# First pass of a two-layer attention block: full-array products of a step in one row, sums of exponentials counted a step later

## The chip, the cores and the metric

The kernel runs on one core of one Trainium2 chip. The metric is the device time of the program in microseconds. The median of three runs of the kernel before is 4034.56 us (4032.42 to 4036.78).

## What is computed

The input x has 8 images of 256 channels and 64 x 64 pixels, in float32. Two layers follow each other. The first, which the change concerns, is attention with keys and values from a reduced image:

```python
xr = conv(x, w_sr, stride 4)            # 256 tokens per image
xr = layer norm of xr over channels
q = w_q @ x
k, v = split(w_kv @ xr)
sim = q . k / sqrt(32)                  # 8 heads of 32 channels, 4096 queries, 256 keys
out = softmax(sim) @ v
x2 = x + gamma * (w_out @ out)
```

The second layer is linear attention on x2: a product with `w_qkv` (768 x 256), a 5 x 5 depthwise convolution with a small mixing, sums of k times v, their application to q, and a projection that is added to x2.

## The kernel before, in words

The program has three passes. `first_pass` does the first layer, the product with `w_qkv`, and some preparation of weights; `second_pass` does the convolution and the sums; `third_pass` applies them. A fourth part, `general`, is run only if sums in the softmax were out of range, which these data never bring. Engines are called PE (TensorE), DVE (VectorE), ACT (ScalarE), POOL (GpSimd) and SP (SyncE, which issues the DMAs).

The first pass walks through 256 steps. The list `order` runs over image `b` (8), block `s` of 512 pixels (8), half `c` of the channels, that is four heads (2), and half `kc` of the keys, that is 128 (2). So an image is a batch of 32 steps, even steps have kc = 0 and odd steps kc = 1, and two steps make one (s, c). The work is spread over steps as in a pipeline. In step n, with m = n - 1:

- `scores` (L770) multiplies q by k for step n. Each of four heads uses 32 rows of the array (L774, tile `sc`); the four results take four of the five PSUM banks that carry the tag `mm`. ACT takes the exponentials (L780) into tiles `e`, of which there are 12, that is three steps.
- `valued` (L788) multiplies the exponentials of step m by v (L793). Each head uses 32 columns of the array. The result `av` has a PSUM bank of its own and collects both halves of the keys.
- `joined` (L802), in odd steps, lets POOL add the exponentials of both halves, head by head (L804), into those of the first half.
- `counted` (L806), when m is odd, multiplies these by a matrix of ones, 32 columns per head (L809). The result `den`, also in a PSUM bank of its own, holds the sums of the exponentials, each 32 times.
- `normed` (L811) follows at once: ACT copies av to `att` (L817); DVE transposes den (L819), takes the reciprocal of one copy of each sum (L820), spreads it back by a transpose (L822) and multiplies att by it (L824). Two small ACT activations (L830) note the sums for the range check; they are put into the list `late`.
- `queries` makes q for the step after next, in even steps (L759, copied by ACT at L767).
- `added` (L836), in every fourth step, for the block whose last scores came three steps before, multiplies two att by `w_out` (L840, four full-array products in two banks `mm`), adds x on DVE (L841) and stores x2.
- After every second block, `differences` (L850) and the seven products of `qkv` (L870), three times over, are put into the table `todo`, for the next seven steps with 2, 3, 4, 1, 4, 3 and 4 products (the 21 products of a Strassen scheme). Their results, in banks `mm`, are copied by ACT (L947) or combined by DVE (L898, L901, L954, L958, L967), and partly transposed (L905, with a copy to `stage` at L911); both transposes and stores go through `late`. `new_stage` (L862) gives the buffer of a plane, whose border POOL clears (L864, L865).
- `keys_values` (L675) makes keys and values of the next image. It is a generator and is advanced in steps 12 to 26 of each batch, with the strided convolution (L687, tile `sr`) in the first eight of these.
- `conv_weights` (L654) prepares weights of the second pass in the first 32 steps: DVE multiplies into the one buffer `wb` (L663), which is stored by DMA.

What stands in `late` is run after the next step's scores. The products in `todo` come before `valued` in odd steps and after it in even steps. The instructions of each engine are issued in the order of this loop, except where the framework's scheduler moves them; `keep_in_program_order` marks those that it may not move. A read of a tile waits for its write by a semaphore, and a new use of a buffer waits for the last reader of the old one.

Of the kernel before, what the change touches and what calls it, by code (L numbers as in the profile page):

```python
# [27 lines left out]
F32 = mybir.dt.float32  # L28
AF = mybir.ActivationFunctionType
ALU = mybir.AluOpType  # L30
AX = mybir.AxisListType

P = 128
# [12 lines left out]
QB = 512  # L46
# [528 lines left out]
def first_pass(ctx: ExitStack, tc: tile.TileContext, a, fine, planes, x2d, kd, vd, wtd):  # L575
    nc = tc.nc
# [8 lines left out]
    rest = ctx.enter_context(tc.tile_pool(name="rest", bufs=2))  # L585
# [14 lines left out]
    def load_x(b):  # L600
        x_tiles[b] = xpools[b % 2].tile([P, 2, HW], F32, tag="x", name=f"x_{b}")
        for s in range(NG):
            load_strip(b, s)
# [42 lines left out]
    def border(b):  # L646
        v = vd[b].rearrange("n y x e -> y x n e")
        src = nil.rearrange("p (n e) -> p n e", n=8)
        for i in (0, NB2 + 1):
            nc.sync.dma_start(v[i], src)  # L650
            nc.sync.dma_start(v[1 : NB2 + 1, i], src[:NB2])
# [104 lines left out]
    def queries(b, s, c):  # L756
        ps = bank(f"q_{b}_{s}_{c}")
        for ci in range(2):
            nc.tensor.matmul(  # L759
                ps,  # L760
                consts["wq"][:, ci, c * P : (c + 1) * P],
                x_tiles[b][:, ci, s * QB : (s + 1) * QB],
                start=(ci == 0),
                stop=(ci == 1),
            )
        qs = two.tile([P, QB], F32, tag="q", name=f"q_{b}_{s}_{c}")
        nc.scalar.copy(qs, ps)  # L767
        return qs

    def scores(b, s, c, kc, qs):  # L770
        scs = [bank(f"sc_{b}_{s}_{c}_{kc}_{h}") for h in range(4)]
        for h in range(4):
            rows = slice(h * D0, (h + 1) * D0)
            nc.tensor.matmul(  # L774
                scs[h], kks[b][rows, c, kc * P : (kc + 1) * P], qs[rows], start=True, stop=True
            )
        es = []
        for h in range(4):
            e = two.tile([P, QB], F32, tag="e", name=f"e_{b}_{s}_{c}_{kc}_{h}", bufs=E_BUFS)
            nc.scalar.activation(e, scs[h], AF.Exp, scale=D0**-0.5)  # L780
            es.append(e)
        return es

    sums = {}

    late = []

    def valued(b, s, c, kc, es):  # L788
        if kc == 0:
            sums["av"] = psum_early.tile([P, QB], F32, tag="av", name=f"av_{b}_{s}_{c}")  # L790
        for h in range(4):
            cols = slice(h * D0, (h + 1) * D0)
            nc.tensor.matmul(  # L793
                sums["av"][cols],
                vvs[b][:, kc, c * P + h * D0 : c * P + (h + 1) * D0],
                es[h],
                start=(kc == 0),
                stop=(kc == 1),
            )


    def joined(es0, es1):  # L802
        for h in range(4):
            nc.gpsimd.tensor_tensor(es0[h], es0[h], es1[h], ALU.add)  # L804

    def counted(b, s, c, es):  # L806
        sums["den"] = psum_early.tile([P, QB], F32, tag="den", name=f"den_{b}_{s}_{c}")
        for h in range(4):
            nc.tensor.matmul(sums["den"][h * D0 : (h + 1) * D0], ones_w, es[h], start=True, stop=True)  # L809

    def normed(b, s, c):  # L811
        av, den = sums["av"], sums["den"]
        i = 2 * ((b * NG + s) * 2 + c)
        att = rest.tile([P, QB], F32, tag="att", name=f"att_{b}_{s}_{c}", bufs=4)
        turn = rest.tile([P, NB, D0], F32, tag="rden", name=f"rden_{b}_{s}_{c}", bufs=1)
        one = two.tile([P, NB], F32, tag="one", name=f"one_{b}_{s}_{c}")
        nc.scalar.copy(att, av)  # L817

        nc.vector.transpose(turn.rearrange("p n d -> p (n d)"), den)  # L819
        nc.vector.reciprocal(one, turn[:, :, 0])  # L820
        r = rest.tile([P, NB, D0], F32, tag="rall", name=f"rall_{b}_{s}_{c}", bufs=1)
        nc.vector.transpose(r, one.unsqueeze(2).to_broadcast([P, NB, D0]))  # L822
        r = r.rearrange("p n d -> p (n d)")
        nc.vector.tensor_mul(att, att, r)  # L824

        def noted():
            for k, t in enumerate((turn[:, :, 0], one)):
                copy = two.tile([P, NB], F32, tag="copy", name=f"copy_{b}_{s}_{c}_{k}")
                tc.keep_in_program_order(
                    nc.scalar.activation(copy, t, AF.Copy, accum_out=seen[:, i + k : i + k + 1])  # L830
                )

        late.append(noted)
        return att

    def added(b, s, att, oc):  # L836
        xt, cols = x_tiles[b], slice(s * QB, (s + 1) * QB)
        ps = bank(f"o_{b}_{s}_{oc}")
        for c in range(2):
            nc.tensor.matmul(ps, consts["wout"][:, c, oc * P : (oc + 1) * P], att[c], start=(c == 0), stop=(c == 1))  # L840
        nc.vector.scalar_tensor_tensor(  # L841
            xt[:, oc, cols], ps, consts["gam"][:, 0:1], xt[:, oc, cols], ALU.mult, ALU.add
        )
        nc.sync.dma_start(x2d[b][oc * P : (oc + 1) * P, cols], xt[:, oc, cols])
# [5 lines left out]
    def differences(b, g):  # L850
        xt = x_tiles[b]
        x = xt[:, :, 2 * g * QB : 2 * (g + 1) * QB].rearrange("p c (h n) -> p c h n", h=2)
        b11, b12, b21, b22 = (x[:, c, h] for c in range(2) for h in range(2))
        t = halves.tile([P, 4, QB], F32, tag="differences", name=f"differences_{b}_{g}", bufs=1)
        t1, t2, t3, t4 = (t[:, i] for i in range(4))
        nc.vector.tensor_sub(t1, b12, b11)
        nc.vector.tensor_sub(t2, b22, t1)
        nc.gpsimd.tensor_tensor(t3, b22, b12, ALU.subtract)
        nc.vector.tensor_sub(t4, t2, b21)
        quarters[b, g] = b11, b21, b22, t1, t2, t3, t4  # L860
# [126 lines left out]
    first = queries(0, 0, 0)  # L987
# [1 line left out]
        pass  # L989
    load_x(1)  # L990
    order = [(b, s, c, kc) for b in range(B) for s in range(NG) for c in range(2) for kc in range(2)]
    q, es, att = {0: first}, {}, {}
    ahead = iter(())

    def qkv_lazy(b, g, pair):
        made = []

        def go(i):
            def run():
                if i == 0:  # L1000
                    made.extend(qkv(b, g, pair))
                made[i]()

            return run

        return [go(i) for i in range(7)]

    n_all = len(order)
    todo = {}
    for n in range(n_all + 16):  # L1010
        m = n - 1
        if n < n_all:
            b, s, c, kc = order[n]
            es[n] = scores(b, s, c, kc, q[n // 2])
        was, late[:] = list(late), []
        for f in was:
            f()


        if n % 2:  # L1020
            for f in todo.pop(n, ()):
                f()
        if 0 <= m < n_all:
            valued(*order[m], es[m])
        for f in todo.pop(n, ()):
            f()
        if n < n_all and kc == 0 and n + 2 < n_all:
            q.pop(n // 2 - 1, None)
            q[n // 2 + 1] = queries(*order[n + 2][:3])
        if 0 <= m < n_all and order[m][3] == 1:  # L1030
            counted(*order[m][:3], es.pop(m - 1))
            es.pop(m)
            att[order[m][:3]] = normed(*order[m][:3])
        if n < n_all and kc == 1:
            joined(es[n - 1], es[n])
        if n >= 6 and (n - 6) % 4 == 0 and (n - 6) // 4 < B * NG:
            b, s = (n - 6) // 4 // NG, (n - 6) // 4 % NG
            for oc in range(2):
                added(b, s, [att[b, s, 0], att[b, s, 1]], oc)
            if s % 2:  # L1040
                differences(b, s // 2)
                products = [p for pair in (1, 2, 0) for p in qkv_lazy(b, s // 2, pair)]
                for i, count in enumerate((2, 3, 4, 1, 4, 3, 4)):
                    todo[n + 1 + i] = products[:count]
                    products = products[count:]
        next(weights, None)
        if n < n_all:
            b, at = n // 32, n % 32
            if at == 2:
                border(b)  # L1050
            if b + 1 < B:
                if at == 10 and b > 0:
                    load_x(b + 1)
                if at == 12:
                    ahead = keys_values(b + 1)
                if 12 <= at < 20:
                    next(ahead)
                    next(ahead)
                elif at >= 20:
                    next(ahead, None)  # L1060
# [688 lines left out]
```

## Time and profile before

| | |
|---|---|
| median of three runs | 4034.56 us |
| profiled execution, its own time | 4043.45 us |
| its span (first to last instruction) | 4041.7 us |
| busy: PE / DVE / ACT / POOL | 3954.6 / 2250.5 / 1511.8 / 1275.2 us |
| first score row of batches 1 to 7 | 321.9, 583.6, 840.7, 1098.0, 1355.1, 1612.3, 1869.6 us |
| first and last score row of the pass | 54.0 and 2088.3 us |
| additions of exponentials, L804 | 512 of 1.27 us (median) |

A float32 product of 512 columns appears as two records of a weight load (PEld) and two of a matmul (PE). The timeline joins records of one form that follow each other: a line has the start in us, the time from first start to last end, engine, line, operation, output and inputs, the part of the array used (128*128 is all of it, 32*128 a quarter of the rows, 128*32 a quarter of the columns), the tile's shape and the number of records; in brackets stand the idle time before it and what ended that. The list of waits has who waited for whom, then the sum in us, how often, and the longest. The lines by stretch give start and end, the length, busy time and instructions of PE, weight load, DVE, ACT and POOL, then the granted clock, the share of the DMA engines and GB/s. The page's slices cut the span into 40 parts and give tenths.

### The profile page before, as it was taken

The page shows a single profiled execution, that of the slowest core. Times are in us where ns is not written, and L with a number is a line of the kernel's source. Part 1 is how long each engine was busy: PE and PEld are TensorE (multiplying, and loading weights), DVE is VectorE, ACT ScalarE, POOL GpSimd, SP SyncE. Part 2 cuts the span into 40 slices and gives each one's busy share as a digit, 9 for nine tenths or more (in the row PEclk, how much of TensorE's full clock was granted, in tenths as well). Part 3 has the DMA queues.
Part 4 walks back from the last instruction along what each step waited for, and adds up shares of the span by engine and source line. Part 5 has one row for each costly group of instructions (what it writes and reads, how often), then busy time and mean ns, then how long its engine had stood idle before and what let it go on. Part 6 is the DMA issues. An engine that isn't in the chain of part 4 may idle for free. (4 is left out here: it accounts for less than half of the span.)

```text
span 4041.7 us, 70298 instructions
## 1 busy us (share of the span) xinstructions
PE 3954.6 (98%) x27074; PEld 2260.2 (56%) x27074; DVE 2250.5 (56%) x3752; ACT 1511.8 (37%) x3473; POOL 1275.2 (32%) x1394
## 2 busy tenths in 40 slices
PE   8999999999999999999997999999999998999999
PEld 4333433434334343343335888888888886556555
DVE  2576465564655645555664566666666664444443
ACT  2334344343443434434432222222222223555444
POOL 2334233343343433424433344444444440000000
PEclk9999999999999999999998999999999998999999
DMA  7655444435344353434548878778778756767674
GB/s 236 186 172 144 143 105 145 103 98 155 93 141 112 96 157 93 134 105 107 137 111 237 247 223 235 221 219 236 222 219 233 208 167 173 229 197 235 196 235 138
DMA packets 569897, 691.37 MB, mean 171 GB/s; under 512 B 60112, under 2 KB 429264, under 8 KB 565328
## 3 DMA queue, kind: packets, MB, share of 16 engines
q1 hardware_dynamic: 569552, 686.78, 60.0%
q8 instruction: 215, 3.52, 0.4%
q14 instruction: 130, 1.06, 0.1%
HBM read 412.54 MB, written 274.10 MB: 170 GB/s over the span
## 5 line engine op out<-in xcount | busy, mean ns | idle before, releaser
L804 POOL TENSOR_TENSOR e<-e,e 128x512 f32<-128x512 f32 x512 | 656.2, 1315 | 867.0 <-PE av L793 867.0
L780 ACT ACTIVATE e<-sc 128x512 f32<-128x512 f32 x1024 | 530.6, 602 | 939.1 <-PE sc L774 939.1
L1205 PE MATMUL cv<-w,c 128*128 128x128 f32 x3072 | 386.5, 280 | 9.7 <-POOL c L1149 9.7
L1205 PEld LDWEIGHTS cv<-w,c 128*128 128x128 f32 x3072 | 361.1, 193 | 40.6 <-issue 30.3
L774 PE MATMUL sc<-q,kk 32*128 32x512 f32 x2048 | 312.9, 642 | 11.7 <-DVE x L841 5.3
L1572 DVE TENSOR_TENSOR y<-z,xs 128x256 f32<-128x256 f32 x256 | 142.6, 644 | 316.3 <-ACT z L1563 291.0
L1247 PE MATMUL sums<-vq,r 128*32 128x288 f32 x4096 | 308.3, 414 | 0.0
L885 PE MATMUL qkv<-differences,combined 128*128 128x512 f32 x576 | 306.4, 623 | 1.9 <-DVE whole L901 1.0
L819 DVE STREAM_TRANSPOSE rden<-den 128x512 f32<-128x512 f32 x128 | 91.7, 716 | 369.6 <-PE den L809 369.5
L793 PE MATMUL av<-e,vv 128*32 128x512 f32 x2048 | 275.2, 610 | 0.0
L1221 ACT ACTIVATE r<-s 128x512 f32<-128x512 f32 x256 | 160.5, 627 | 293.5 <-DVE s L1220 289.9
L1209 PE MATMUL cv<-c,w 128*128 128x128 f32 x2048 | 253.4, 277 | 0.0
L1554 PE MATMUL p<-att,wproj 128*128 128x512 f32 x512 | 249.9, 610 | 1.9 <-ACT att L1537 1.9
L1563 ACT ACTIVATE z<-p,bn 128x256 f32<-128x256 f32 x256 | 133.8, 578 | 314.8 <-PE p L1554 241.3
L687 PE MATMUL sr<-x,wsr 128*128 128x256 f32 x1024 | 238.3, 387 | 7.7 <-DMA wsr<-in_w_sr_dram 7.7
L759 PE MATMUL q<-x,wq 128*128 128x512 f32 x512 | 245.3, 601 | 0.2 <-DVE whole L901 0.2
L1554 PE MATMUL p<-agg,wproj 128*128 128x512 f32 x512 | 242.3, 596 | 0.0
L1212 ACT COPY both<-cv 128x512 f32<-128x512 f32 x128 | 75.0, 586 | 444.3 <-PE cv L1205 386.8
L1209 PEld LDWEIGHTS cv<-c,w 128*128 128x128 f32 x2048 | 239.7, 192 | 0.0
L840 PE MATMUL o<-att,wout 128*128 128x512 f32 x512 | 237.7, 605 | 0.0
L687 PEld LDWEIGHTS sr<-x,wsr 128*128 128x128 f32 x1024 | 193.2, 192 | 73.8 <-issue 40.8
L1220 DVE TENSOR_TENSOR s<-cv,both 128x512 f32<-128x512 f32 x256 | 172.1, 673 | 87.6 <-PE cv L1209 43.5
(143 smaller groups left out, 6123.4 us busy)
## 6 DMA issues: line engine op xcount, KB each, us to landing
vq<-v SPq DMA_DIRECT2D x256, 384.0 KB
planes<-stage SPq DMA_DIRECT2D x128, 578.0 KB
d<-planes SPq DMA_DIRECT2D x128, 578.0 KB
raw<-planes SPq DMA_DIRECT2D x128, 272.0 KB
x<-in_xp_dram SPq DMA_DIRECT2D x64, 512.0 KB
wsr<-in_w_sr_dram SPq DMA_DIRECT2D x128, 256.0 KB
x<-x SPq DMA_DIRECT2D x128, 256.0 KB
k<-turned SPq DMA_DIRECT2D x256, 128.0 KB
```

The source lines that it names most:

```text
L687: nc.tensor.matmul(ps[:, oc], w[:, ci, oc * P : (oc + 1) * P], xt[:, ci, f * NK : (f + 1) * NK], start=(f == ci == oc == 0), stop=(f == R ...
L759: nc.tensor.matmul(ps, consts["wq"][:, ci, c * P : (c + 1) * P], x_tiles[b][:, ci, s * QB : (s + 1) * QB], start=(ci == 0), stop=(ci == 1),)
L774: nc.tensor.matmul(scs[h], kks[b][rows, c, kc * P : (kc + 1) * P], qs[rows], start=True, stop=True)
L780: nc.scalar.activation(e, scs[h], AF.Exp, scale=D0**-0.5)
L793: nc.tensor.matmul(sums["av"][cols], vvs[b][:, kc, c * P + h * D0 : c * P + (h + 1) * D0], es[h], start=(kc == 0), stop=(kc == 1),)
L804: nc.gpsimd.tensor_tensor(es0[h], es0[h], es1[h], ALU.add)
L840: nc.tensor.matmul(ps, consts["wout"][:, c, oc * P : (oc + 1) * P], att[c], start=(c == 0), stop=(c == 1))
L885: nc.tensor.matmul(ps, w, x, start=True, stop=True)
L1205: nc.tensor.matmul(out, x, m, start=(da == 0), stop=(da == 1))
L1209: nc.tensor.matmul(out, m, x, start=(da == 0), stop=(da == 1))
L1247: nc.tensor.matmul(ps[h * D0 : (h + 1) * D0, : 36 * D1].rearrange("p (r n e) -> p r n e", r=3, e=D1), kt[:, par, h, 2 * r + c], vq[:, r : ...
L1554: nc.tensor.matmul(ps.rearrange("p (f q n) -> p f q n", f=4, q=4), wproj[:, j, oc * P : (oc + 1) * P], src, start=(j == 0), stop=(j == 3),)
```

## The change

Four things are changed in `first_pass`, and nothing elsewhere.

1. The loop's order. In odd steps of which the position n % 32 is not 12 to 25, the products in `todo` still come before `valued`, and what they put into `late` is now run at once (a second `catch_up`). In the other odd steps they come after `valued` and `counted`, where the products of the next batch's keys follow. In even steps they come after `valued`, as before, and no longer have `counted` between the queries and `added`.
2. `counted` and `normed` are called two steps behind the scores (d = n - 2) instead of one, and so in odd steps; `counted` stands right behind `valued`.
3. `joined` is called in the even step, after `valued` of the odd step before, and adds into the exponentials of the second half; those of the first half are let go then.
4. The copy of av to att is taken out of `normed` and is called (`copied`) right after the second `valued`. The transpose of den is kept in program order.

```diff
+    def catch_up():
+        was, late[:] = list(late), []
+        for f in was:
+            f()
...
     def joined(es0, es1):
         for h in range(4):
-            nc.gpsimd.tensor_tensor(es0[h], es0[h], es1[h], ALU.add)
+            nc.gpsimd.tensor_tensor(es1[h], es0[h], es1[h], ALU.add)
...
+    def copied(b, s, c):
+        att[b, s, c] = rest.tile([P, QB], F32, tag="att", name=f"att_{b}_{s}_{c}", bufs=4)
+        nc.scalar.copy(att[b, s, c], sums["av"])
+
     def normed(b, s, c):
-        av, den = sums["av"], sums["den"]
+        den = sums["den"]
...
-        nc.scalar.copy(att, av)
-
-        nc.vector.transpose(turn.rearrange("p n d -> p (n d)"), den)
+        tc.keep_in_program_order(nc.vector.transpose(turn.rearrange("p n d -> p (n d)"), den))
...
-        was, late[:] = list(late), []
-        for f in was:
-            f()
-
-
-        if n % 2:
+        catch_up()
+
+
+        last = n < n_all and kc == 1 and not 12 <= n % 32 <= 25
+        if last:
             for f in todo.pop(n, ()):
                 f()
+            catch_up()
         if 0 <= m < n_all:
             valued(*order[m], es[m])
+            if order[m][3] == 1:
+                copied(*order[m][:3])
+                joined(es.pop(m - 1), es[m])
+        d = n - 2
+        if 0 <= d < n_all and order[d][3] == 1:
+            counted(*order[d][:3], es.pop(d))
         for f in todo.pop(n, ()):
             f()
         if n < n_all and kc == 0 and n + 2 < n_all:
             q.pop(n // 2 - 1, None)
             q[n // 2 + 1] = queries(*order[n + 2][:3])
-        if 0 <= m < n_all and order[m][3] == 1:
-            counted(*order[m][:3], es.pop(m - 1))
-            es.pop(m)
-            att[order[m][:3]] = normed(*order[m][:3])
-        if n < n_all and kc == 1:
-            joined(es[n - 1], es[n])
+        if 0 <= d < n_all and order[d][3] == 1:
+            normed(*order[d][:3])
```

More of the change, by code (lines that the diff above doesn't have):

```diff
@@ L782, in scores @@
         return es
-    sums = {}
+    sums, att = {}, {}
     late = []
+    def catch_up():
+        was, late[:] = list(late), []
+        for f in was:
+            f()
     def valued(b, s, c, kc, es):
@@ L809, in counted @@
             nc.tensor.matmul(sums["den"][h * D0 : (h + 1) * D0], ones_w, es[h], start=True, stop=True)
+    def copied(b, s, c):
+        att[b, s, c] = rest.tile([P, QB], F32, tag="att", name=f"att_{b}_{s}_{c}", bufs=4)
+        nc.scalar.copy(att[b, s, c], sums["av"])
     def normed(b, s, c):
-        av, den = sums["av"], sums["den"]
+        den = sums["den"]
         i = 2 * ((b * NG + s) * 2 + c)
-        att = rest.tile([P, QB], F32, tag="att", name=f"att_{b}_{s}_{c}", bufs=4)
         turn = rest.tile([P, NB, D0], F32, tag="rden", name=f"rden_{b}_{s}_{c}", bufs=1)
         one = two.tile([P, NB], F32, tag="one", name=f"one_{b}_{s}_{c}")
-        nc.scalar.copy(att, av)
-        nc.vector.transpose(turn.rearrange("p n d -> p (n d)"), den)
+        tc.keep_in_program_order(nc.vector.transpose(turn.rearrange("p n d -> p (n d)"), den))
         nc.vector.reciprocal(one, turn[:, :, 0])
@@ L823, in normed @@
         r = r.rearrange("p n d -> p (n d)")
-        nc.vector.tensor_mul(att, att, r)
+        nc.vector.tensor_mul(att[b, s, c], att[b, s, c], r)
         def noted():
@@ L833, in normed @@
         late.append(noted)
-        return att
     def added(b, s, att, oc):
@@ L991, in first_pass @@
     order = [(b, s, c, kc) for b in range(B) for s in range(NG) for c in range(2) for kc in range(2)]
-    q, es, att = {0: first}, {}, {}
+    q, es = {0: first}, {}
     ahead = iter(())
```

## The prediction

> **What bounds the kernel now.** I read the page first (engine shares, slices), then busy time by stretch, then TensorE's (PE's) timeline of some 30 us, then the list of waits.
>
> ```profile
> PE 3954.6 (98%) x27074; PEld 2260.2 (56%) x27074; DVE 2250.5 (56%) x3752; ACT 1511.8 (37%) x3473; POOL 1275.2 (32%) x1394
> ...
> PEclk9999999999999999999998999999999998999999
> ```
> ```profile
> 750.00:1000.00 250.00, 249.16 (x1064) 96.56 (x1063) 140.23 (x214) 102.94 (x249) 90.60 (x99) 1.00 0.44 121
> 1000.00:1250.00 250.00, 249.15 (x1068) 94.40 (x1067) 137.64 (x213) 105.87 (x258) 91.41 (x100) 1.00 0.44 118
> ```
>
> In the first pass PE is busy 249 of 250 us at full clock, no other engine over 56%, DMA 44%. So PE's queue is the path. A busy PE is not a PE at its peak, so I read its rows from start to start:
>
> ```profile
> 895.70 1.07 PE L793 MATMUL av<-e,vv 128*32 128x512 f32 x8
> 896.69 1.14 PE L774 MATMUL sc<-q,kk 32*128 32x512 f32 x8
> 897.76 1.06 PE L793 MATMUL av<-e,vv 128*32 128x512 f32 x8
> 898.76 1.98 PE L885 MATMUL qkv<-x,wqkv 128*128 128x512 f32 x4
> 900.58 1.02 PE L885 MATMUL qkv<-differences,combined 128*128 128x512 f32 x2
> 901.44 1.88 PE L759 MATMUL q<-x,wq 128*128 128x512 f32 x4
> 903.25 1.07 PE L809 MATMUL den<-e,ones_w 128*32 128x512 f32 x8
> 904.24 1.14 PE L774 MATMUL sc<-q,kk 32*128 32x512 f32 x8
> ...
> 911.01 1.06 PE L793 MATMUL av<-e,vv 128*32 128x512 f32 x8
> 912.01 1.98 PE L759 MATMUL q<-x,wq 128*128 128x512 f32 x4
> 913.92 1.06 PE L809 MATMUL den<-e,ones_w 128*32 128x512 f32 x6
> 915.14 1.04 PE L809 MATMUL den<-e,ones_w 128*32 128x512 f32 x2 [0.16 <-POOL e L804]
> 916.12 3.70 PE L840 MATMUL o<-att,wout 128*128 128x512 f32 x8
> 919.75 1.14 PE L774 MATMUL sc<-q,kk 32*128 32x512 f32 x8
> ```
>
> A product of 512 columns is two records. I call full-array rows F, score rows (32*128) S, column-tiled rows (128*32: av, den) V. In F a record takes 0.4275 us and the row 0.21 once: 10 records from 898.76 to 903.25 are 4.49 = 4.275 + 0.21. A V row of four products takes 1.00 = 0.855 + 0.14, an S row 1.07 = 0.855 + 0.215. The odd 0.14 or 0.21 is paid wherever the kind changes. The den row at 913.92 takes 2.20 instead of 1.00: it waits for GpSimd's (POOL's) addition. What may go wrong stands in the waits (the last line from those of 54 to 260 us alone):
>
> ```profile
> POOL e L804 <- PE av L793: 867.0, 128, 16.8
> ...
> POOL stage L864 <- DMA planes<-stage: 209.8, 68, 11.7
> ```
> ```profile
> DVE wb L663 <- DMA wt<-wb: 48.0, 15, 5.5
> ```
>
> **What the Trainium skill says.** "TensorEngine Tiling (Array Packing)", Key Properties: "Changing tiling mode (not just tile) drains the TensorE". The trace agrees, with 0.14 to 0.215 us per change. "TensorE: Matmul & The Clock Gate", The mechanism: tiles in different column groups run concurrently; here four products in 0.855 us, the time of one. The same page, Architectural detail: every engine but PE works strictly in order; so POOL's memset at L864, waiting for a store, holds back the additions behind it. "SBUF — State Buffer", Terms: VectorE (DVE) and GpSimd exclude each other from a shared port pair; additions at L804 take 1.27 us at the median and 2.81 at most, so they are sometimes held up.
>
> **The change, part by part.** Steps alternate, even (kc 0) and odd (kc 1). Before: even S V F den F, odd S F V, with products of the next batch's keys as a further F row in steps 12 to 20. After: even S V F; odd S F V+den, and S V+den F in steps 12 to 25 of a batch. No product is added or removed.
>
> *Rows.* I counted runs of one kind in the programs' order. Each of batches 1 to 6 goes from 48 V and 49 F to 32 and 32, S stays 32: 16 den rows join av rows, 17 F rows join others. The joined V row's price is shown once, at the end of the pass, where two av sets stand together:
> ```profile
> 2093.03 1.92 PE L793 MATMUL av<-e,vv 128*32 128x512 f32 x16
> ```
> The next row starts at 2094.88: 1.85 = 1.71 + 0.14, so joining saves all of one 0.14. Saved per batch: 16 x 0.14 = 2.24, and 17 x 0.21 = 3.57. If only half of it came, 2.9 per batch would be lost; more than the whole isn't possible.
>
> *Waits of den.* In a batch, three den rows take 2.20 and two 1.36 instead of 1.00 (the step before is short: the additions, four of 1.24, begin at the odd step's V and end 5.2 us later). That is 3 x 1.2 + 2 x 0.36 = 4.3. After, they begin when the even step's av is done (they write what av reads), and den stands behind F, S, av of later rows: at the least 4.49 + 1.07 + 1.0 = 6.6 us on (step 20), mostly 10. So the wait goes, with 1.4 us to spare. Late next is the exponential of the odd step, whose buffer (12 of them, three steps) the addition frees: it starts at 5.8 and its fourth at 7.6, after additions that end 1.5 to 5.2. No wait.
>
> *normed, a step later but nearer its user.* Its chain on DVE (transpose, reciprocal, transpose, product) takes 2.48 us (904.46 to 906.94 in DVE's timeline). It used to have two steps until `added` takes att, now one. The worst odd step queues seven DVE operations of 0.7 ahead of it: counted from that step's S, V+den ends at 6.55, DVE gets to the chain at 7.6 and ends at 10.1; o starts at 6.55 + 1.07 + 1.0 + 0.21 + 3 x 0.86 = 11.4. Covered with 1.3 to spare; uncovered, each us is paid by up to 64 o rows. A small gain: the chain no longer sits just ahead of the o evictions, which now hold S and F some 0.1 to 0.2 us three times a batch: 0.4.
>
> *copied* moves the copy of av up ACT's queue, behind the four exponentials and two small copies and ahead of the copies of products. Same work (0.62 us); ACT is 41% busy; 0. The small copies (L830) now wait for the chain of the step before; queued behind them are the copies of part (DVE needs them in the same F row) and of q (needed a step later); but the chain's reciprocal is done at 8.6 in the count above and the exponentials ahead end at 9.8, so they don't wait; 0. POOL's additions (sixteen groups of four a batch) stay. SP's DMAs are the same in number; stores of stage go out slightly earlier through the second catch_up. Passes two and three keep their order but for under ten lines at the seam.
>
> *First batch.* 14 V and 14 F rows less (4.9) and den waits of 9.7 (excess over 1.00, added up from the timeline) make 14.6. But there DVE, in order, waits for the weights' stores (L663: 48 us above), and o and den's bank hang on DVE. The trace has no step of it without that wait: from 0 (also some loss) to 14.6; I take 4.
>
> *Last batch.* 16 V, 8 F (3.9); den waits 10.0, among them 2.1 and 1.6 at the very end. New: the last addition starts only after the last av, 5.0 against 2.8 of F between: 2.3 back. 11.6.
>
> **Sum.** 6 x (2.24 + 3.57 + 4.3 + 0.4) = 63; + 4 + 11.6 = 79 us. The profiled execution took 4043.45 (span 4041.7), 9 over the median; less 79 it would be 3964. On the median of 4034.56: 3956.
>
> **Rivals.** (1) *o waits for att*: the one-step reach is too short. For: slack of 1.3 against additions that swell to 2.8. Against: 56% DVE. One us at the 32 o rows behind long steps: -47, 3988. (2) *Joined rows save nothing* (the drain is per instruction group): -79 + 39 = -40, 3995. Against: the x16 row. (3) *The first pass's start gains all*: -90, 3945. (4) *Slower: POOL's queue.* In steps 6 and 30 of each batch the memset of stage (L864) stands ahead of the additions and waits for the store of the same buffer. In the count above that V row ends at 8.6, the fourth exponential after it is due at 17.9, and the additions take 5.0: a landing up to 4.3 us after the V row costs nothing; past that each us delays exponentials and PE, 16 times. I expect 3.6: the store is issued at some 7.2, when ACT and DVE have finished the block, and lands 5.0 later, as from 884.96 to the memset at 889.94 now. At the longest wait seen, 11.7, it would cost 7.4 x 16 = 118: +39, 4074. It decides from 9.2 us on. Against: in the timeline these waits are 1.5 to 7 us of which most passes before V.
>
> **Chances.** Forecast 0.74; (1) 0.11; (2) 0.05; (3) 0.06; (4) 0.02; a mixture near no change 0.02. The range, 3938 to 3985, takes the forecast's own (first batch 0 to 14.6; 0.1 us of unseen waits in each of 256 steps, 26) and (3), and leaves (1)'s worse half and the rest out. Below 0.2% (8 us) the measurement can't tell from no change: faster 0.95, same 0.02, slower 0.03.
>
> **What would show it.** Batches 257.1 us apart (first score row to first score row, 583.55 to 840.67) should come to 246 to 247. Rows V x16 of 1.85; no POOL release in den's rows but at the end; F rows of q and o in one; first batch (54.0 to 321.9) least changed. Wrong if o rows show idle time before DVE att, if exponentials wait for POOL, or if x16 rows exceed 2.0.

## The result, and the profile after

The changed kernel took 3971.2 us (median of four runs, 3966.8 to 3977.6) against 4034.5 us for the kernel before (four runs, 4032.4 to 4036.8): a ratio of 0.984, 95% interval 0.983 to 0.986. That is 63 us less, where 79 was forecast. The time lies in the forecast's range. The profiled execution of the changed kernel took 3977.62 us (span 3975.8), 65.8 less than the profiled one of before.

First the page, its engine shares and the clock's slices:

```profile
PE 3884.2 (98%) x27074; PEld 2279.0 (57%) x27074; DVE 2267.2 (57%) x3752; ACT 1516.5 (38%) x3473; POOL 1291.5 (32%) x1394
...
PEclk9999999999999999999998999999999999999999
```

The numbers of instructions are the same as before; PE is still 98% busy. Busy time by stretch in the first pass (columns as before: PE, weight load, DVE, ACT, POOL, then clock, DMA share and GB/s):

```profile
750.00:1000.00 250.00, 249.61 (x1101) 103.74 (x1100) 143.86 (x218) 106.56 (x258) 96.78 (x103) 1.00 0.46 124
```

This view can't show the gain as idle time that went: PE was "busy" 249 of 250 us before, and is now. It shows it as work per time: 1101 matmul records in 250 us instead of 1064. The gain was inside the busy time, at the seams (the places where PE goes from one kind of row to another), and the timeline of PE (start, duration, what, number of records) shows it there:

```profile
799.33 1.88 PE L891 MATMUL qkv<-x,wqkv 128*128 128x512 f32 x4
801.14 1.07 PE L798 MATMUL av<-e,vv 128*32 128x512 f32 x8
802.02 1.04 PE L814 MATMUL den<-e,ones_w 128*32 128x512 f32 x8
802.99 1.14 PE L774 MATMUL sc<-q,kk 32*128 32x512 f32 x8
...
805.06 1.13 PE L891 MATMUL qkv<-differences,combined 128*128 128x512 f32 x2
806.02 1.88 PE L759 MATMUL q<-x,wq 128*128 128x512 f32 x4
807.74 3.60 PE L846 MATMUL o<-att,wout 128*128 128x512 f32 x8
811.27 1.14 PE L774 MATMUL sc<-q,kk 32*128 32x512 f32 x8
```

Av and den now take 1.85 us together (801.14 to 802.99): 1.71 for the products, 0.14 once, where they took 1.00 each. The F row of 14 records from 805.06 (products, q and o) ends at 811.27: 6.21 = 14 x 0.4275 + 0.22. From the second batch on no den row waits for POOL but the very last. In the list of waits of the whole execution:

```profile
POOL e L809 <- PE av L798: 879.1, 103, 16.8
...
POOL stage L870 <- DMA planes<-stage: 140.7, 38, 10.6
...
POOL stage L870 <- ACT copy L837: 73.7, 8, 9.3
```

POOL still waits for av, which is its place in the order; in steady batches (2 to 6, counted from 0) no PE row is late for it. Its wait for the stores of `stage` fell from 210 to 141 us, but eight waits for ACT's small copies (L837) came in, 74 us, so its queue stands about as long in all.

The length of a batch, first score row to first score row, is the finest measure: within one execution, batches 2 to 6 agree to 0.5 us or better, while passes two and three took 1899.9 to 1909.4 us in the executions shown here, so that single times can't tell a few us. "End" is from the pass's last score row to the first matmul of `total`; "last" is batch 7, to its last score row.

| us | start | batch 0 | 1 | 2 to 6, each | last | end | time of the profiled run |
|---|---|---|---|---|---|---|---|
| before | 54.0 | 267.9 | 261.6 | 257.1 to 257.4 | 218.7 | 44.2 | 4043.45 |
| after | 52.7 | 264.4 | 252.4 | 248.2 to 248.4 | 209.6 | 45.9 | 3977.62 |
| saved | 1.3 | 3.5 | 9.2 | 8.9 | 9.1 | -1.7 | 65.8 |
| forecast | | 4 | 10.5 | 10.5 | 11.6 with the end | | 79 |

### The profile page after: what moved, and what is told of

It is laid out like the page before. It is cut to its first block, busy times and chain, and to the rows that moved or that the text cites. A ratio compares the mean times of both kernels' runs of the same rounds, so it can differ in the third digit from the quotient of the medians.

```text
span 3975.8 us, 70172 instructions
## 1 busy us (share of the span) xinstructions
PE 3884.2 (98%) x27074; PEld 2279.0 (57%) x27074; DVE 2267.2 (57%) x3752; ACT 1516.5 (38%) x3473; POOL 1291.5 (32%) x1394
## 5 line engine op out<-in xcount | busy, mean ns | idle before, releaser
L809 POOL TENSOR_TENSOR e<-e,e 128x512 f32<-128x512 f32 x512 | 679.3, 1357 | 941.9 <-PE av L798 879.1
L907 DVE TENSOR_TENSOR whole<-part,qkv 128x512 f32<-128x512 f32 x256 | 175.5, 687 | 193.1 <-PE qkv L891 181.9
```

The source lines that it names most:

```text
L809: nc.gpsimd.tensor_tensor(es1[h], es0[h], es1[h], ALU.add)
```

## The experiments

The theory after the result: rows and den's waits brought what the forecast said (5.8 and 4.3 us per batch), and the 1.6 us that are missing per batch are waits of score rows for PSUM banks that DVE gives back late, at places that the forecast didn't have. Rivals: that a joined row saves less than one whole seam, and that the first batches hold the difference. All edits but those shown last were run once, so the lengths of batches decide, not the times. The kernel before took 4040.03 beside the four edits of den amid the products, den's waits, step 24 and the last batch, and 4036.90 beside the other three.

**den back between two F rows.** This puts the seams back and nothing else: 9 odd steps of a batch get one V row and one F row more.

```diff
+        d = n - 2
         if last:
-            for f in todo.pop(n, ()):
+            fs = todo.pop(n, [])
+            for f in fs[: len(fs) // 2]:
+                f()
+            if 0 <= d < n_all and order[d][3] == 1:
+                counted(*order[d][:3], es.pop(d))
+            for f in fs[len(fs) // 2 :]:
                 f()
...
-        d = n - 2
-        if 0 <= d < n_all and order[d][3] == 1:
+        if d in es and 0 <= d < n_all and order[d][3] == 1:
             counted(*order[d][:3], es.pop(d))
```

> The changed kernel, but in the nine odd steps of a batch that have products before av, den is put amid these products: nine V rows and nine F rows more per batch, same instructions, no new wait by the count (additions end 5.2 us after the av before, den comes at 7.5). Theory (each change of kind costs 0.14 or 0.21): 9 x 0.35 = 3.15 us per batch, 248.2 becomes 251.4, in time +25. Rival (joining rows saved nothing, the gain is all waits): 248.2, time unchanged.

Measured: batches 2 to 6 of 251.3 to 251.7 us, 3.1 more than in the changed kernel; the time was 3987.21. PE's timeline of this run:

```profile
801.74 1.07 PE L814 MATMUL den<-e,ones_w 128*32 128x512 f32 x8
802.74 1.98 PE L891 MATMUL qkv<-x,wqkv 128*128 128x512 f32 x4
804.65 1.07 PE L798 MATMUL av<-e,vv 128*32 128x512 f32 x8
805.65 1.14 PE L774 MATMUL sc<-q,kk 32*128 32x512 f32 x8
```

Den alone takes 1.00 again (801.74 to 802.74), and the products behind it pay their own 0.2 (four records in 1.91 instead of 1.71). Nine times 0.14 + 0.21 is 3.15. A batch of this run has 41 V and 41 F rows instead of 32 and 32, and what its rows take above their price is the same in sum (3.1 us in batch 2, in the changed kernel too). So the price of a seam is real, and the rival that joined rows save nothing, or half, falls.

**Den's waits alone.** The kernel before, with its order of rows; POOL adds into tiles of its own as soon as both exponentials are there, so that den needn't wait (the 12 exponentials become 9 to make room).

```diff
...
-            nc.gpsimd.tensor_tensor(es0[h], es0[h], es1[h], ALU.add)
+            e = two.tile([P, QB], F32, tag="sum", name=f"sum_{n}_{h}", bufs=4)
+            nc.gpsimd.tensor_tensor(e, es0[h], es1[h], ALU.add)
...
-            counted(*order[m][:3], es.pop(m - 1))
+            counted(*order[m][:3], both.pop(m))
```

> The kernel before, with its rows and its order, but the additions are written into four tiles of their own (12 buffers of exponentials become 9 to make room). They no longer wait for av, only for the exponentials, and so end before den needs them. Theory: den's waits go and nothing else: batches 257.1 - 4.3 = 252.8, rows still 48 V and 49 F, in time some -35 with the ends of the pass (4000). Rival 1 (the waits of den are cover for something else that is late anyway): 257. Rival 2 (fewer buffers make exponentials wait): above 253, with waits of ACT for POOL in the trace.

Measured: 4040.36, no gain; batches 2 to 6 of 255.6 to 256.1 instead of the 252.8 expected. So each of these gained 1.4 us of the 4.3, and batches 0 and 1 lost 4.2 and 7.2 against the profile of before; why, stays open. The expectation failed, and the failure taught more than the rest. Den's waits did go: what V rows take above their price is 0.04 us per batch instead of 4.37. But score rows of steps 2, 6, 10 and 30 now wait 0.62 to 0.64 us each, and further rows 0.2 to 0.7. The second rival's sign shows too: three times a batch an exponential waits some 0.65 us for POOL. It isn't what delays PE, for no V row, which takes the exponentials, is late (the 0.04 above). The timeline of all engines around the score row of step 2:

```profile
859.45 5.42 POOL L806 TENSOR_TENSOR sum<-e,e 128x512 f32<-128x512 f32 x4 [8.21 <-ACT e L780]
859.55 1.71 DVE L828 TENSOR_TENSOR att<-att,rall 128x512 f32<-128x512 f32 x1
861.18 0.68 DVE L962 TENSOR_TENSOR part<-part,qkv 128x512 f32<-128x512 f32 x1
...
863.15 0.68 DVE L971 TENSOR_TENSOR part<-part,qkv 128x512 f32<-128x512 f32 x1
863.25 1.76 PE L774 MATMUL sc<-q,kk 32*128 32x512 f32 x8
863.89 0.29 PEld L774 LDWEIGHTS sc<-q,kk 32*128 32x128 f32 x2 [0.33 <-DVE part L971]
```

DVE's multiplication of att, two operands in SBUF, starts 0.1 us after POOL's additions and takes 1.71 us instead of 0.69. The combinations of products behind it in DVE's queue each take their usual 0.68 (one of their operands is in PSUM), but they all come 1.0 later; the last of them ends at 863.83, and the fourth head's score product, which needs that bank, starts then. The same stands at steps 6, 10 and 30: L828 takes 1.64 to 1.71, and a score product waits for DVE. So a wait of PE for POOL was exchanged for one of PE for DVE.

The Trainium skill, page "SBUF — State Buffer", section "Who interferes with whom", says that a DVE instruction with two SBUF inputs contends with a GpSimd one that reads SBUF, and that one with a single SBUF input, outside the modes that use two ports, doesn't. The trace agrees: of the DVE lines above only L828 is stretched. POOL's four additions read singly tell more. The first ended at 860.71, and L828 ended 0.55 us after it (861.26); the second took 1.72 where the others took 1.27 to 1.28:

```profile
860.67 1.72 POOL L806 TENSOR_TENSOR sum<-e,e 128x512 f32<-128x512 f32 x1
```

So L828 was held for most of the first addition and then let in ahead of the second, which was held in turn. That it is a port that holds them is the page's word; the trace shows only the durations. The kernel before had the same in small: its third difference on DVE (L859, two SBUF operands) takes 1.64 us beside POOL's own difference (L858), where L856 and L857 take 0.69. So the profile of before could have warned of it.

**The same in the changed kernel.** There DVE's first difference (L862, two SBUF operands) falls beside POOL's additions. The timeline of all engines in step 3, after the change:

```profile
833.20 5.23 POOL L809 TENSOR_TENSOR e<-e,e 128x512 f32<-128x512 f32 x4 [7.71 <-PE av L798]
834.82 3.60 PE L846 MATMUL o<-att,wout 128*128 128x512 f32 x8
836.74 0.75 DVE L847 SCALAR_TENSOR_TENSOR x<-o,gam,x 128x512 f32<-128x512 f32 x1 [3.11 <-PE o L846]
837.52 1.45 DVE L862 TENSOR_TENSOR differences<-x 128x512 f32<-128x512 f32 x1
838.35 1.14 PE L774 MATMUL sc<-q,kk 32*128 32x512 f32 x8
838.90 0.74 DVE L847 SCALAR_TENSOR_TENSOR x<-o,gam,x 128x512 f32<-128x512 f32 x1
839.69 1.98 PE L891 MATMUL qkv<-x,wqkv 128*128 128x512 f32 x4 [0.20 <-DVE x L847]
```

The difference takes 1.45 instead of 0.69 and ends 0.55 us after POOL's last addition (838.42), and the second eviction of o, queued behind it, frees its bank some 0.4 us after it could have; the products behind the scores, which need that bank, start 1.34 after the scores instead of 1.07. The test keeps both evictions of o ahead of the difference:

```diff
-        nc.vector.scalar_tensor_tensor(
-            xt[:, oc, cols], ps, consts["gam"][:, 0:1], xt[:, oc, cols], ALU.mult, ALU.add
+        tc.keep_in_program_order(
+            nc.vector.scalar_tensor_tensor(
+                xt[:, oc, cols], ps, consts["gam"][:, 0:1], xt[:, oc, cols], ALU.mult, ALU.add
+            )
         )
...
-        nc.vector.tensor_sub(t1, b12, b11)
+        tc.keep_in_program_order(nc.vector.tensor_sub(t1, b12, b11))
```

> The changed kernel, but both evictions of o are kept ahead of the first of the differences on DVE. In the changed kernel this difference, which reads two operands from SBUF, takes 1.45 us instead of 0.69 while GpSimd adds exponentials (it did not overlap them before), and the second eviction, which frees a bank for the scores of steps 3 and 11, stands behind it: 0.27 us twice a batch. Theory (port shared by the two engines, and the order behind it): these two waits go, 248.2 becomes 247.7 or 247.8; the difference still takes longer than 0.69. Rival (the eviction is late because o ends late): 248.2, waits unchanged.

Measured: 247.7 to 247.9, as expected, and the waits of steps 3 and 11 are gone; single time 3977.66. The timeline of all engines of this run at the same place:

```profile
843.12 0.75 DVE L848 SCALAR_TENSOR_TENSOR x<-o,gam,x 128x512 f32<-128x512 f32 x1 [3.12 <-PE o L846]
...
844.73 1.14 PE L774 MATMUL sc<-q,kk 32*128 32x512 f32 x8
844.84 0.75 DVE L848 SCALAR_TENSOR_TENSOR x<-o,gam,x 128x512 f32<-128x512 f32 x1 [0.96 <-PE o L846]
845.50 0.68 DVE L864 TENSOR_TENSOR differences<-x 128x512 f32<-128x512 f32 x1
```

DVE now idles for 0.96 us ahead of the second eviction, and is on time. In one point the expectation missed: the difference, which now comes after POOL's additions, is back at 0.68. Idle time on an engine that isn't the bound was worth 0.5 us a batch to the one that is.

**Step 24.** In steps 12 to 25 the changed order has V+den ahead of the products of odd steps. At step 24 that leaves only a short product of the next image's keys (`rs`) between the products of step 23 and the scores. The timeline of the changed kernel:

```profile
758.71 0.69 DVE L907 TENSOR_TENSOR whole<-part,qkv 128x512 f32<-128x512 f32 x1 [0.17 <-PE qkv L891]
759.31 0.68 DVE L973 TENSOR_TENSOR part<-part,qkv 128x512 f32<-128x512 f32 x1
759.37 0.61 PE L726 MATMUL rs<-ident,wide 128*128 128x128 f32 x4
759.90 2.30 PE L774 MATMUL sc<-q,kk 32*128 32x512 f32 x8
760.35 0.68 DVE L907 TENSOR_TENSOR whole<-part,qkv 128x512 f32<-128x512 f32 x1
761.08 0.29 PEld L774 LDWEIGHTS sc<-q,kk 32*128 32x128 f32 x2 [0.74 <-DVE whole L907]
```

The fourth head's product waits for a bank until DVE's combination (L907) with the last product ends at 761.03; the score row takes 2.23 (759.90 to av at 762.13) instead of 1.07. The test ends the range of steps with V+den first at 19, and leaves it out in the last batch:

```diff
-        last = n < n_all and kc == 1 and not 12 <= n % 32 <= 25
+        last = n < n_all and kc == 1 and (n >= n_all - 32 or not 12 <= n % 32 <= 19)
```

> As e1, and in all batches the other order holds for steps 12 to 19 alone, where the strided convolution's products stand. The steps after it then have a further full-array row for mean, rs and v. Theory: three F rows more, 3 x 0.21 = 0.6 us per batch, against the wait of 1.16 us before the scores of step 24, which the av row covers again: 248.2 becomes 247.7. Rival (that wait only moves to the next row that needs a bank): 248.8.

Measured: 247.6 to 247.9. PE's timeline of this run at the same step: `rs` stands behind av and den, and the scores behind it take 1.07.

```profile
764.58 1.04 PE L814 MATMUL den<-e,ones_w 128*32 128x512 f32 x8
765.55 0.71 PE L726 MATMUL rs<-ident,wide 128*128 128x128 f32 x4
766.19 1.14 PE L774 MATMUL sc<-q,kk 32*128 32x512 f32 x8
```

It costs three F rows more (3 x 0.21 = 0.63) and takes the wait of 1.16 away: 0.53, and 0.4 to 0.6 were measured.

**The last batch alone.** It makes no keys for a next image, but the changed kernel keeps the order made for them. So behind the odd steps 12 to 25 the scores follow the products at once. Score rows of steps 16, 17, 18, 24, 25 and 26 wait 0.54 to 0.57 us each, of 21 and 27 0.34 and 0.43, together 4.1 (those of 17 and 25 stand behind an even step's products, and are released by DVE too). One of them, in PE's timeline of the changed kernel:

```profile
1918.06 1.71 PE L774 MATMUL sc<-q,kk 32*128 32x512 f32 x8
1919.70 1.07 PE L798 MATMUL av<-e,vv 128*32 128x512 f32 x8
```

```diff
-        last = n < n_all and kc == 1 and not 12 <= n % 32 <= 25
+        last = n < n_all and kc == 1 and (n >= n_all - 32 or not 12 <= n % 32 <= 25)
```

> The changed kernel, but in the last batch (which prepares no further keys) the products stand before av in all odd steps. Theory (a score row right behind products waits until DVE has emptied their banks; the av row between them used to cover that): the waits of score rows in steps 16 to 27 of the last batch, 4.1 us together, go, and from its first to its last score row it takes 205.6 us instead of 209.6; the other batches stay at 248.2. Rival (the waits come from the chain of normed, which now runs in every even step, whatever the order): 209.6 again. In time 4 us, which is within the scatter of single runs, so the trace decides.

Measured: last batch 206.0 against 209.6. Of the 4.1 us, 3.6 went; steps 19 and 27 keep 0.27 each, as steps 3 and 11 do. The time of 3959.12 is lower than that explains: passes two and three took 1901.6 us in this execution and 1909.4 in the one of the changed kernel, and batches 0 and 1, which the edit doesn't touch, 6.5 less.

**The first batch.** The forecast put most of what may be gained there (14.6) behind DVE's waits for the weights. So both kernels were run with this edit, which was to halve the pace of the preparation of weights:

```diff
-        next(weights, None)
+        if n % 2 == 0:
+            next(weights, None)
```

> The kernel before, but the second pass's weights are prepared in every second step, so over 64 steps instead of 32, all of them as before. Theory (in the first batch DVE, in order, stands behind the store of the one buffer wb, and PE behind DVE): the first batch gets shorter, from 267.9 us toward the later ones' 257.1, and the second stays near 261. Here den's waits and rows are as before. Rival (the first batch is slow for another reason, as its longer loads): 268.

> The changed kernel with the weights in every second step. Theory: with DVE's waits for wb rarer, the first two batches save, against the same edit of the kernel before, more than the 3.4 and 9.2 us (12.6) of the plain pair: near 2 x 8.9 or up to 14.6 + 9. Rival (the joined rows bring nothing before the products of qkv have begun, whatever DVE does): 12 or less again. Batches 2 to 6 stay at 248.2.

Measured, batches 0 and 1: the kernel before 272.3 and 259.4, the changed one 252.0 and 250.5 (times 4040.94 and 3961.40). The pair differs by 29 us in these two batches, more than the 24 that the theory allowed at most, because batch 0 of the kernel before didn't come down at all. But the two runs don't test the theory, for the pace was not halved. By the end of batch 0 the traces have 26 and 25 of the 32 multiplications into `wb`, against 31 and 30 without the edit; the edited loop asks for 16 in those steps, and DVE's instructions did not keep to its pace. DVE's waits ahead of them between 52 and 325 us, in the order before, changed, before with the edit, changed with the edit:

```profile
DVE wb L663 <- DMA wt<-wb: 53.8, 19, 5.5
...
DVE wb L663 <- DMA wt<-wb: 45.8, 16, 7.1
...
DVE wb L663 <- DMA wt<-wb: 44.9, 17, 6.3
...
DVE wb L663 <- DMA wt<-wb: 33.8, 13, 7.1
```

Most of the waits stayed. In the changed kernel o of step 11, which stood 6.9 us behind att while DVE waited for a load of weights (L659), no longer waits with the edit; o of step 6 still does, 4.4 us.

Batch 0 also differs by more than edits explain: 264.4 and 263.0 for the changed kernel, 259.5 with the edit of the last batch, which doesn't touch it, and 274.1 and 273.6 with the edits of step 24 and of the evictions, which shorten the steady batches. So the 3.5 us that the pair of profiles shows say nothing sure of what the change gains there, not even the sign. The 252.0 with the slower weights lies below all of these; which of DVE's waits makes that isn't shown.

**Both corrections together, and the changed kernel again,** five runs each on one chip.

> The changed kernel with the edits of e2 (the other order in steps 12 to 19 alone, none in the last batch) and e7 (evictions of o first). Theory: -0.5 for the one and -0.4 for the other per batch (247.3), last batch -3.5 or more, so 8 to 10 us less than the changed kernel (3961 to 3963 against 3971). Rival (what the two edits free is taken by the next wait): same as the changed kernel.

> The changed kernel, unaltered, on the same chip as e8, for the comparison: 63 us under the kernel before (ratio 0.984), batches 2 to 6 at 248.2; shows how far the first batch and passes two and three differ between executions.

Measured: together 3967.1 us (3964.7 to 3970.5), ratio to before 0.983, interval 0.981 to 0.984; the changed kernel again 3972.3 (3966.4 to 3976.9), ratio 0.984, interval 0.982 to 0.985. In the batches the two corrections add up: 247.1 in each of batches 2 to 6 (1.1 less), 204.9 in the last (4.7 less), 10 us in these six. The profiled run gives 5 of them back in batch 0 (268.0 against 263.0). The medians are 5.2 us apart, where 8 to 10 were expected, and the intervals overlap: this version is likely a little faster than the changed kernel, and the times alone don't settle it.

## Why the forecast was right, and where it fell short

The mechanism was right, and the size came out a fifth short (63 for 79): steady batches stand 248.2 to 248.4 us apart, where the forecast named 246 to 247. By its steps:

- **Rows** (2.24 + 3.57 per batch): right. 48 V and 49 F rows became 32 and 32, the joined row takes 1.85, and putting 18 seams back cost 3.1 us, where the prices give 3.15.
- **Waits of den** (4.3): right. V rows exceed their price by 0.08 us per batch, before by 4.37. The claim of 1.4 us to spare held in every steady batch.
- **The 0.4 for the evictions of o** ("the chain no longer sits just ahead of the o evictions"): this term came to nothing. Score rows of steps 4, 12 and 27 did lose their waits, 0.5 us in all. But POOL's additions came to lie beside DVE's difference, which is stretched and holds the second eviction: steps 3 and 11 wait 0.27 each, before 0.13. The run with the evictions first gave 0.5 back.
- **No term for the banks at step 24**: a whole step was missing. The forecast counted the rows of steps 12 to 25 but didn't ask what stands between the products and the scores once av has moved ahead of them. 1.16 us per batch.

  Together: at the forecast's prices (0.4275 us a record, and 0.215, 0.21 and 0.14 for a row of S, F and V), S and F rows stood 1.84 us per batch above their price before. After, they stand 1.90 above it, and 3.06 with step 24. 5.81 + 4.3 - 1.22 = 8.9, as measured; the forecast had 10.5. In the profiled pair, where 13 us are missing, six batches make 9 of them.
- **Last batch** (11.6): 7.4 with the end. The same missing question costs most of the 4.1 there, 3.6 by the edit of the last batch. The last den waits 2.9, the forecast had 2.3 and its reason was right. PE's timeline of the changed kernel there:

```profile
2030.71 2.25 PE L814 MATMUL den<-e,ones_w 128*32 128x512 f32 x6
2033.59 1.04 PE L814 MATMUL den<-e,ones_w 128*32 128x512 f32 x2 [0.64 <-POOL e L809]
```

- **First batch** (4, between 0 and 14.6): 3.5. The value was chosen, not derived, and batch 0 varies by more than that between runs, so its nearness is luck. One part of the working was wrong: the 14.6 let all of den's waits there (9.7) go. The rows of V+den in steps 3, 5 and 9, with no products yet to stand ahead of them, take 6.3 us above their price, and POOL's additions release them. PE's timeline of the changed kernel has step 5:

```profile
72.06 1.07 PE L798 MATMUL av<-e,vv 128*32 128x512 f32 x8
72.94 1.03 PE L814 MATMUL den<-e,ones_w 128*32 128x512 f32 x4
75.01 1.05 PE L814 MATMUL den<-e,ones_w 128*32 128x512 f32 x2 [1.03 <-POOL e L809]
76.23 1.05 PE L814 MATMUL den<-e,ones_w 128*32 128x512 f32 x2 [0.18 <-POOL e L809]
77.21 1.14 PE L774 MATMUL sc<-q,kk 32*128 32x512 f32 x8
```

  What DVE's waits for the weights cost PE in this batch stays open.
- **copied, the small copies, POOL's memsets** at nothing: right for PE, of which no row in a steady batch waits for them. POOL does wait behind the small copies (the 74 us above), which the forecast didn't have.

The rivals. (1), o waiting for att, is seen, but only in the first batch, where DVE waits for the weights. The page's costliest groups of the changed kernel (busy time and mean, then idle time before and its releaser) have it:

```profile
L846 PE MATMUL o<-att,wout 128*128 128x512 f32 x512 | 234.4, 600 | 11.9 <-DVE att L831 11.9
```

These are three waits, all in batch 0. In steady batches o never waits for att: the slack of 1.3 us was enough. (2), joined rows save nothing, is refuted by the run with den amid the products. (3), the first batch gains all, didn't happen: the steady batches hold most of the gain. (4), POOL's queue, didn't happen either: the longest wait for a store was 10.6 us, and no exponential was late for PE behind it in a steady batch. The time fell halfway between the forecast's 3956 and rival (1)'s 3988, but what is missing is not rival (1)'s wait.

## What to carry to other kernels

On a queue that is always "busy", read rows from start to start, count changes of kind, and price each: here 0.14 to 0.2 us a seam, 33 seams a batch. When rows are moved, ask for each row of scores or products not only whether its inputs are there but which row used to cover the return of its output banks. And before work is given to GpSimd, or moved in time there, ask which DVE instructions with two SBUF operands it will lie beside, and what is queued behind them.

## What was not expected of the hardware

- A DVE operation of two SBUF operands (128x512, float32) takes 0.69 us alone and 1.45 to 1.71 beside POOL's additions. From 325 to 1870 us the mean of the first difference (L856 before, L862 after) rose from 0.69 to 1.30 us, that of the att multiplication from 0.69 to 0.80. POOL's additions rose only from 1.28 to 1.32. Operations with a PSUM operand kept 0.68 to 0.75 beside the same additions.
- Two column-tiled rows of different inputs and PSUM banks join as fully as two of the same: 1.85 us, the first four products of den starting 0.88 after those of av.
- Passes two and three, untouched by all edits, took 1899.9 to 1909.4 us in different executions: a spread larger than most of the effects studied here.
